# A graph network kernel on one core: a new SBUF layout for the second network's first loads, and an earlier place for a rarely taken branch

## The chip, the cores and the metric

The kernel runs on 1 core of one Trainium2 chip. The metric is the device time of one execution in microseconds. Before the change the median of 3 runs is 2925.94 us (2923.68 to 2931.75). The profile was taken on another execution, which took 2932.24 us; its span, from the first to the last recorded instruction, is 2930.4 us.

## What is computed

The reference runs two networks on 16 graphs (batches b) of 1024 nodes with 128 features. The first network weighs each graph's adjacency by the cosine of the node features; the second thins the adjacency once ("dilation") and runs three layers of a neighbour mean on it, with a normalization over all batches after each layer. Between the two stands a residual and a layer normalization, `h0`.

```python
# first network, three layers
h = h @ W + b
nh = h / max(norm(h), EPS)
h = (edge_weight * (nh @ nh.T)) @ h          # relu but for the last layer
# dilation: row by row over the adjacency, earlier rows' removals count for later rows
row = carry[n]; num = sum(row); rank = cumsum(row)
rm = row & (rank % sf == 0)                  # sf from num
carry[n] = row & ~rm; carry[:, n] &= ~rm
# second network, three layers, adj_d = adj * keep
deg = clip(sum(adj_d, -1), 1)
out = (adj_d @ x / deg) @ Wr + x @ Wx + b
h_l = batchnorm(relu(out / norm(out)))
y = concat(h1, h2, h3) @ Wl + bl             # plus the residual
```

## The kernel before

All batches are held as 8 chunks of 128 nodes (`NCH = 8`), so an adjacency is an 8 by 8 field of 128x128 blocks. The instructions of each engine are put in an order by a scheduler from the program text and its priorities; each engine then works through its own queue in order. SP issues the loads, POOL issues most of the stores.

Stage A, from the start to about 1730 us, is one `ExitStack` (`actx`) with the pools `pool1` ("a1", single buffers) and `pool2` ("a2", double buffers). Two things are woven together in it. `layer0()` (the kernel's name for the first network) works on two batches at a time through three layers; its steps are `products` (cosines times adjacency, L324 to L336), `turn` (transposes, L353), `sums` and `sums_back` (L364, L378), and at a batch's end `residual` (L392, with the DVE operation at L401 and the store of `x2` at L404) and `next_layer` (layer normalization, the store of `h0` at L410). The adjacency of the two batches in work lies in `adjA` (L217). The generator `dilation()` makes the keep masks row chunk by row chunk in a fast form that guesses a number of rounds, and stores them in HBM as `keep` (L720). It also counts in `astray` whether any guess failed. Its tiles (`patt`, `an`, `kl`, `T`, `Z`, `E`, `rank`, `kp` and small ones) are taken from `pool1` and `pool2`, among those of the first network. The driver at L743 weaves the two until `dilation()` ends, with some 7% of the first network left (`SPREAD`).

Then the count is summed (L749 to L754) and each engine loads it into a register (L755, `values_load`). `while step0(): pass` (L766) issues the rest of the first network. After that `tc.If(n_off > 0)` (L768) holds an exact dilation, 16 long loops which run only where a guess failed; with these inputs it isn't taken, so every engine jumps over it. Last come the residual and `h0` of batch 15 (L771, L772).

Stage B, from there on, opens its own pools: "res" (`hR`, the layer's result for all batches), "b2", "br" (the adjacency blocks `aT0` to `aT7`), for its first layer also "bk" (`kb`, the keep mask of a batch, 8 loads of 256 KB into one tile of two buffers; and `both`). A pool of stage B is laid where pools of stage A were, and its first tile waits for what was there.

The first layer of stage B (L908 to L997; called the second layer in the change's name) does for each batch: `fetch` (L913) loads `kb` and `hN` (the batch's `h0`); `weighted` (L791) multiplies it by the weights (`pt_h`, `pw` L803); for each of 8 chunks `masked` (L921) loads the adjacency and its transpose into `aT` (L924, L928), makes the symmetric mask `both` (L933, L935) and applies it (L941, L945), `turn` (L950) transposes the upper blocks and stores `aT` to HBM as `adT` (L960), `Sums.add` (L827) accumulates `agg` (L831). The two other layers (L1040 on) read `adT` back (L1047). The projections of all layers gather in `acc` (L1002), a pool opened after the first layer.

Of the kernel before, what the change touches and what calls it, by code (L numbers as in the profile page):

```python
# [16 lines left out]
P = 128  # L17
# [29 lines left out]
def tile_adj_preln_d2(  # L47
# [47 lines left out]
    GT = 4  # L95
# [73 lines left out]
    with ExitStack() as actx:  # L169
        pool1 = actx.enter_context(tc.tile_pool(name="a1", bufs=1))  # L170
# [5 lines left out]

        w0 = pool1.tile([P, 3, P], F32, name="w0")
# [37 lines left out]


        adjA = pool1.tile([P, 2, base(NCH), P], F32, name="adjA")  # L217
        Nat = {}

        def adj_place(b, q):  # L220
            return adjA[:, b % 2, base(q) : base(q + 1), :]

        def adj_piece(b, q):
            Nat[b, q] = nat = pool2.tile([P, NCH, P], F32, tag="nat", name=f"nat_{b}_{q}")
            nc.sync.dma_start(
                nat[:, : NCH - q, :], adj[b][q * P :, q * P : (q + 1) * P].rearrange("(c p) q -> p c q", p=P)
            )
# [280 lines left out]
        patt = pool1.tile([P, SLOTS, N + 2], F16, name="patt")  # L508
        nc.gpsimd.memset(patt[:, :, 0:2], 0.0)

        astray = pool1.tile([P, BH], F32, name="astray")
        nc.vector.memset(astray, 0.0)

        def thresholds(x, nm):


            th = pool2.tile([P, 2, BH], F32, tag="th", name=f"th_{nm}")
            nc.vector.tensor_scalar(th[:, 0, :], x, EVENS, None, ALU.add)
            nc.vector.tensor_scalar(th[:, 1, :], x, float(T_DIL), LOW, ALU.is_le, ALU.mult)
            return th[:, 0, :], th[:, 1, :]  # L520
# [6 lines left out]
        def dilate(k, half, exact):  # L527
# [8 lines left out]
            left = pool2.tile([P, BH], F32, tag="left", name=f"left{nk}")  # L536
            rest = pool2.tile([P, BH], F32, tag="rest", name=f"rest{nk}")
            if k == 0:
                nc.vector.memset(left, 0.0)
            rbias = pool2.tile([P, BH], F32, tag="rbias", name=f"rbias{nk}")  # L540
            T = pool2.tile([P, BH, P], F16, tag="T", name=f"T{nk}")
            for i in range(BH):
                b = half * BH + i
                an = pool2.tile([P, N], F32, tag="an", name=f"an{nk}_{i}")
                nc.sync.dma_start(an, adj[b, cols, :])
                on = pattern(i)[:, 2 + k * P :]
                nc.scalar.activation(on, an[:, k * P :], AF.Sign)
                nc.scalar.activation(on, on, AF.Relu, accum_out=rest[:, i : i + 1])
                if k:
                    pk = pool2.tile([P, NCH - 1, P], F16, tag="kl", name=f"kl{nk}_{i}")  # L550
                    nc.sync.dma_start(
                        pk[:, :k, :].rearrange("p j q -> p (j q)"), keep_d[b][: k * P, cols], transpose=True
                    )
                    nc.vector.scalar_tensor_tensor(
                        pattern(i)[:, 2 : 2 + k * P],
                        an[:, : k * P],
                        0.0,
                        pk[:, :k, :].rearrange("p j q -> p (j q)"),
                        ALU.is_gt,
                        ALU.mult,  # L560
                        accum_out=left[:, i : i + 1],
                    )
                yield 0.75
                if i % GT == GT - 1:
                    four = range(i - GT + 1, i + 1)
                    bs_ = slice(i - GT + 1, i + 1)
                    pdt = ps_sm.tile([P, GT, P], F16, tag="sm", name=f"pdt{nk}_{i}")
                    for n, ii in enumerate(four):
                        nc.tensor.transpose(pdt[:, n, :], pattern(ii)[:, diag], ident16)
                    dT = pool2.tile([P, GT, P], F16, tag="dT", bufs=1, name=f"dT{nk}_{i}")  # L570
                    nc.scalar.activation(dT, pdt, AF.Copy)
                    nc.vector.tensor_scalar(rbias[:, bs_], rest[:, bs_], 2.0, -2.0, ALU.mult, ALU.add)
                    yield 0.1
                    pT = ps_sm.tile([P, GT, P], F32, tag="sm", name=f"pT{nk}_{i}")
                    for n, ii in enumerate(four):
                        nc.tensor.matmul(pT[:, n, :], lhsT=dT[:, n, :], rhs=upto, start=True, stop=False)
                        nc.tensor.matmul(pT[:, n, :], lhsT=pattern(ii)[:, diag], rhs=off, start=False, stop=False)
                        nc.tensor.matmul(pT[:, n, :], lhsT=ident16, rhs=after, start=False, stop=True)
                    for n, ii in enumerate(four):
                        nc.scalar.activation(T[:, ii, :], pT[:, n, :], AF.Identity, bias=rbias[:, ii : ii + 1])  # L580
                    yield 0.1


            x0 = pool2.tile([P, BH], F32, tag="x0", name=f"x0{nk}")
# [5 lines left out]
            Z = pool2.tile([P, BH, P], F16, tag="Z", name=f"Z{nk}")  # L590
            if ends:
                nc.vector.tensor_scalar(Z, T, 0.0, None, ALU.is_equal)
            else:
                found = pool2.tile([P, 1], F32, tag="found", name=f"found{nk}")
                nc.vector.tensor_scalar(Z, T, 0.0, 0.0, ALU.is_equal, ALU.add, accum_out=found)
                nc.vector.tensor_tensor(astray[:, 0:1], astray[:, 0:1], found, ALU.add)
            E = pool2.tile([P, BH, P], F16, tag="E", name=f"E{nk}")
            par = pool2.tile([P, BH], F16, tag="par", name=f"par{nk}")

            def even(x, nm):  # L600

                ev = pool2.tile([P, BH], F32, tag="ev", name=f"ev_{nm}")
                nc.vector.tensor_scalar(ev, x, EVENS, EVENS, ALU.add, ALU.subtract)
                return ev

            def removals(x, nm):


                if exact:
                    f, low = thresholds(x, nm)  # L610
                    at = pool2.tile([P, 2, BH], F32, tag="at", name=f"at_{nm}")
# [8 lines left out]
                else:  # L620
                    ev = even(x, nm)
                    mid = pool2.tile([P, BH], F16, tag="mid", name=f"mid_{nm}")
# [13 lines left out]
            if exact:  # L636
                x = pool1.tile([P, BH], F32, tag="xe", name=f"xe_{nk}")
# [4 lines left out]
            else:  # L642
                x = x0
                for r in range(ROUNDS[k]):
                    was = x
                    pc = removals(x, f"{nk}_{r}")
                    yield 1.0
                    x = pool2.tile([P, BH], F32, tag="x", name=f"x_{nk}_{r}")
                    nc.vector.tensor_tensor(x, x0, pc, ALU.subtract)
                moved = pool2.tile([P, BH], F32, tag="moved", name=f"moved_{nk}")  # L650
                nc.vector.tensor_tensor(moved, was, x, ALU.not_equal)
                nc.vector.tensor_tensor(astray, astray, moved, ALU.add)
            fin = pool2.tile([P, 3, BH], F32, tag="fin", name=f"fin{nk}")
# [9 lines left out]
            else:  # L663
# [9 lines left out]
                small = pool2.tile([P, BH], F32, tag="small", name=f"small{nk}")  # L673
# [20 lines left out]
            for i in range(BH + 1):  # L694
                if i < BH:

                    pt = pattern(i)
                    ranks[i] = rank = pool2.tile([P, N], F16, tag="rank", bufs=3, name=f"rank{nk}_{i}")
                    nc.vector.tensor_tensor_scan(rank, pt[:, 1 : N + 1], pt[:, 2:], 0.0, ALU.add, ALU.add)  # L699
                    yield 2.5  # L700
# [11 lines left out]
                kp = pool2.tile([P, N], F16, tag="kp", name=f"kp{nk}_{i}")  # L712
# [53 lines left out]
        while step0():  # L766
            pass
        with tc.If(n_off > 0):  # L768
            for _ in dilation(exact=True):
                pass  # L770
        batches[-1].residual()  # L771
# [3 lines left out]
    with ExitStack() as bctx:  # L775
        res = bctx.enter_context(tc.tile_pool(name="res", bufs=1))
        pool2 = bctx.enter_context(tc.tile_pool(name="b2", bufs=2))
        poolr = bctx.enter_context(tc.tile_pool(name="br", bufs=1))
# [129 lines left out]
        with ExitStack() as c1:  # L908
            poolk = c1.enter_context(tc.tile_pool(name="bk", bufs=2))
# [3 lines left out]
            def fetch(b):  # L913
                kb = poolk.tile([P, NCH, N], F16, tag="kb", name=f"kb_{b}")
                for c in range(NCH):
                    nc.sync.dma_start(kb[:, c, :], keep_d[b][c * P : (c + 1) * P, :])
                hN = pool2.tile([P, NCH, D], F32, tag="hN2", bufs=1, name=f"hN1_{b}")
# [3 lines left out]
            def masked(b, q, kb):  # L921
# [10 lines left out]
                for c in range(row):  # L932
                    nc.tensor.transpose(pk[:, c, :], kb[:, q + c, q * P : (q + 1) * P], ident16)  # L933
                both = poolk.tile([P, NCH, P], F16, tag="both", name=f"both_{b}_{q}")
# [3 lines left out]
                    kb[:, q, q * P :].rearrange("p (c q) -> p c q", q=P),  # L938
# [61 lines left out]
        poolc = bctx.enter_context(tc.tile_pool(name="bc", bufs=1))  # L1000
        ps_a = bctx.enter_context(tc.tile_pool(name="b_a2", bufs=2, space=PSUM))
        acc = poolc.tile([P, B, NCH, D], F32, name="acc")  # L1002
# [8 lines left out]
        def project(l, b, hT):  # L1011

            for h in range(NHALF):
# [3 lines left out]
                yield h, pp, acc[:, b, h * CPH : (h + 1) * CPH, :]  # L1017
# [11 lines left out]
        def residual(b):  # L1029
# [3 lines left out]
            for c in range(NCH):  # L1033
# [3 lines left out]
                a = acc[:, b, c, :]  # L1037
# [88 lines left out]
```

## Time and profile before

| what | value |
|---|---|
| median of the runs | 2925.94 us |
| profiled execution: time, span | 2932.24 us, 2930.4 us |
| PE busy | 2673.3 us, 91% of the span |
| DVE busy | 1955.9 us, 67% |
| ACT busy | 1420.2 us, 48% |
| POOL busy | 452.9 us, 15% |
| moved by DMA | 585.21 MB, mean 200 GB/s |
| shares of the chain that ended last | PE 56%, DVE 18%, DMA 13%, issue 6% |

The chain that ended last is followed back from the last instruction, at each step to what released it. PE leads it, but the share is a mean over stages with different limits: each stage has to be read from its own windows. "Idle before" in a row of the timeline is the time that the engine stood before this instruction, with the instruction that ended it; a name with q (SPq, PEq, DVEq) is an engine's sequencer. The granted clock (PEclk) is a share of TensorE's full clock.

### The profile page before, as it was taken

To read this page: it belongs to the slowest core of one execution; us is meant where nothing else is said; L and a number is where in the kernel's file an instruction comes from. 1 tells how busy PE (TensorE), PEld (TensorE's weight loads), DVE (VectorE), ACT (ScalarE), POOL (GpSimd) and SP (SyncE) were. 2 spreads that over 40 slices of the span, in tenths; PEclk is the share of its full clock that TensorE was granted. 3 is DMA by queue.
4 is the path that set the end of the run, shared out by engine and by line. 5 is a ranking of instruction groups with operands and counts; after the bars stand their busy time and mean duration, and the time that the engine had idled before them with its cause. 6 is when DMAs were issued, how large, how long until landed. Compare 5 with 4: busy or idle time off the path is not lost.

```text
span 2930.4 us, 51972 instructions
## 1 busy us (share of the span) xinstructions
PE 2673.3 (91%) x18803; PEld 2205.6 (75%) x18803; DVE 1955.9 (67%) x4945; ACT 1420.2 (48%) x4069; POOL 452.9 (15%) x604
## 2 busy tenths in 40 slices
PE   5898998998989989998998979999989999899996
PEld 3666666666666666766666758989979999899996
DVE  2777778877977878788778446777772233455555
ACT  5766667557546546455455323333333333333333
POOL 2111112012011112121112002222220010010010
PEclk9999999999999999999999989999999999999998
DMA  8437258247347456386162039999995666576763
GB/s 268 145 115 219 89 168 247 77 139 229 92 130 219 105 169 188 95 248 176 39 206 105 1 114 403 405 406 404 405 372 173 208 210 202 177 243 222 240 217 115
DMA packets 383017, 585.21 MB, mean 200 GB/s; under 512 B 85201, under 2 KB 267345, under 8 KB 382753
## 3 DMA queue, kind: packets, MB, share of 16 engines
q1 hardware_dynamic: 343280, 425.28, 45.9%
q0 software_dynamic: 38464, 156.07, 14.4%
q8 instruction: 151, 2.47, 0.3%
q14 instruction: 114, 0.93, 0.1%
q10 hardware_dynamic: 1008, 0.46, 0.1%
HBM read 403.44 MB, written 163.58 MB: 193 GB/s over the span
## 4 chain that ended last, share of the span: by engine, by line
PE 56%; DVE 18%; DMA 13%; issue 6%; ACT 4%; POOL 1%; SPq 1%; POOLq 0%; DVEq 0%; another core or an unknown queue 0%; ACTq 0%
PE agg L831 20%; PE po L364 7%; PE pg L324 6%; DVE rank L699 5%; PE pw L803 5%; PE po L378 5%; DVE ew L336 4%; DMA aT<-in_adj_dram 3%; PE gt L353 3%; PE pp L1016 2%; DMA kl<-keep 2%; PE pw L273 2%; DMA an<-in_adj_dram 2%; DMA aT<-adjT 1%; DMA kb<-keep 1%
## 5 line engine op out<-in xcount | busy, mean ns | idle before, releaser
L831 PE MATMUL agg<-hw,aT 128*128 128x128 f32 (+1 forms) x6144 | 742.9, 277 | 8.8 <-DVE aT L941 7.5
L831 PEld LDWEIGHTS agg<-hw,aT 128*128 128x128 f32 x6144 | 712.1, 192 | 14.7 <-DVE aT L941 10.1
L324 PE MATMUL pg<-nhT 128*128 128x512 f32 (+3 forms) x1152 | 457.4, 500 | 71.9 <-DVE ew L336 63.0
L364 PE MATMUL po<-ew,hS 128*128 128x512 f32 (+3 forms) x1152 | 455.3, 499 | 13.8 <-ACT hTo L387 9.9
L336 DVE TENSOR_TENSOR ew<-pg,adjA 128x768 f32<-128x768 f32 (+3 forms) x528 | 425.1, 827 | 4.6 <-DVEq L768 2.7
L378 PE MATMUL po<-ew,hS 128*128 128x128 f32 x2688 | 366.9, 277 | 0.0
L378 PEld LDWEIGHTS po<-ew,hS 128*128 128x128 f32 x2688 | 339.3, 193 | 36.6 <-issue 36.3
L354 ACT ACTIVATE ew<-gt 128x512 f32<-128x512 f32 (+1 forms) x480 | 208.9, 465 | 243.2 <-PE gt L353 240.2
L324 PEld LDWEIGHTS pg<-nhT 128*128 128x128 f32 x1152 | 188.7, 193 | 171.6 <-issue 120.9
L699 DVE TENSOR_TENSOR_SCAN rank<-patt 128x1024 f16<-128x1024 f16 x128 | 294.0, 2307 | 0.9
L364 PEld LDWEIGHTS po<-ew,hS 128*128 128x128 f32 x1152 | 195.8, 194 | 105.6 <-issue 72.9
L353 PEld LDWEIGHTS gt<-ident,ew 128*128 128x128 f32 x1344 | 167.8, 143 | 97.3 <-issue 68.5
L333 DVE TENSOR_TENSOR ew<-pg,adjA 128x128 f32<-128x128 f32 x384 | 108.1, 282 | 196.3 <-PE pg L324 150.9
L353 PE MATMUL gt<-ident,ew 128*128 128x128 f32 x1344 | 212.1, 277 | 4.1 <-ACT ew L354 2.7
L881 POOL TENSOR_TENSOR o<-o,rn 128x512 f32<-128x512 f32 x96 | 107.6, 1121 | 650.4 <-DVE rn L880 646.0
L803 PE MATMUL pw<-wrx,hT 128*128 128x256 f32 x768 | 181.1, 391 | 10.2 <-ACT hT L1006 9.7
L805 DVE TENSOR_TENSOR own<-pw,bs 128x256 f32<-128x256 f32 x192 | 81.4, 424 | 148.0 <-ACT hw L804 148.0
L803 PEld LDWEIGHTS pw<-wrx,hT 128*128 128x128 f32 x768 | 146.3, 196 | 32.7 <-ACT hT L1006 10.5
L959 ACT ACTIVATE aT<-pta 128x512 f32<-128x512 f32 (+3 forms) x160 | 71.2, 466 | 205.0 <-PE pta L958 178.0
L860 DVE SCALAR_TENSOR_TENSOR o<-agg,invdeg,own 128x128 f32<-128x128 f32 x384 | 109.7, 344 | 87.0 <-PE agg L831 78.3
L876 ACT ACTIVATE own<-o 128x128 f32<-128x128 f32 x384 | 114.6, 301 | 103.3 <-DVE o L860 103.2
L301 POOL TENSOR_TENSOR hS<-hN,rn 128x1024 f32<-128x1024 f32 x48 | 94.6, 1970 | 409.2 <-DVE rn L157 300.4
(161 smaller groups left out, 3962.2 us busy)
## 6 DMA issues: line engine op xcount, KB each, us to landing
an<-in_adj_dram SPq DMA_DIRECT2D x128, 512.0 KB, 4.6
keep<-kp POOLq DMA_DIRECT2D x128, 256.0 KB, 3.6
kb<-keep SPq DMA_DIRECT2D x128, 256.0 KB, 5.4
aT<-adT SPq DMA_DIRECT2D x32, 960.0 KB, 5.4
aT<-adT SPq DMA_DIRECT2D x32, 832.0 KB, 5.5
aT<-adT SPq DMA_DIRECT2D x32, 704.0 KB, 4.6
aT<-adT SPq DMA_DIRECT2D x32, 576.0 KB, 3.4
xb<-in_x_dram SPq DMA_DIRECT2D x31, 512.0 KB, 5.1
```

The costliest lines, as they stand in the source:

```text
L324: nc.tensor.matmul(pg[:, :n, :].rearrange("p c q -> p (c q)"), lhsT=self.nhT[:, q * P : (q + 1) * P], rhs=self.nhT[:, (q + c) * P : (q + c ...
L333: nc.vector.tensor_tensor(ew[:, 0, :], pg[:, 0, :], place[:, 0, :], ALU.mult)
L336: nc.vector.tensor_tensor(both[0][:, :, off, :], pg[:, own:n, :].unsqueeze(1).to_broadcast([P, 2, n - own, P]), both[1][:, :, off, :], ALU ...
L353: nc.tensor.transpose(pt[:, i, :], ew[:, at + i, :], ident)
L354: nc.scalar.activation(ew[:, at : at + n, :], pt[:, :n, :], AF.Copy)
L364: nc.tensor.matmul(self.po[:, c * P : (c + n) * P], lhsT=self.hS[:, q, :], rhs=ew[:, c - q : c - q + n, :].rearrange("p c q -> p (c q)"), ...
L378: nc.tensor.matmul(self.po[:, q * P : (q + 1) * P], lhsT=self.hS[:, q + n, :], rhs=ew[:, NCH - 1 - q + n, :], start=False, stop=closes and ...
L699: nc.vector.tensor_tensor_scan(rank, pt[:, 1 : N + 1], pt[:, 2:], 0.0, ALU.add, ALU.add)
L803: nc.tensor.matmul(pw[:, i, :], lhsT=hT[:, 2 * h + i, :], rhs=wrx[:, l, :], start=True, stop=True)
L831: nc.tensor.matmul(self.place(c), lhsT=aT[:, blk, :], rhs=self.hw[:, source, :], start=source == 0 and c % self.ga == 0, stop=ends(c, source),
L860: nc.vector.scalar_tensor_tensor(self.o[:, c, :], self.place(c)[:, :P], invdeg[:, b, c : c + 1], self.own[:, c, :], ALU.mult, ALU.add,)
L876: nc.scalar.activation(self.own[:, n, :], self.o[:, n, :], AF.Square, accum_out=ss[:, c : c + 1])
```

## The change

Five edits:

- A pool `poold` ("ad") is opened ahead of `pool1`, and all tiles of the dilation, and `nat` (the adjacency pieces before they are transposed), move to it.
- `adjA` becomes two tiles, one for even and one for odd batches, and stands first in `pool1`.
- In stage B the order of the pools is turned: "bc" first, then "br", "b2" and "res". `acc` becomes 16 tiles `acc0` to `acc15` of "bc", and the first layer's `kb` (now four tiles of two chunks for each batch), `hN` and `both` take turns with them under the same tags. The pool "bk" is gone.
- The loop that issues the rest of the first network is cut in two: 12 steps, then the branch to the exact dilation, then the remaining steps.
- The final residual's tile `x2f` no longer shares its buffer with `hN`.

```diff
     with ExitStack() as actx:
+        poold = actx.enter_context(tc.tile_pool(name="ad", bufs=2))
         pool1 = actx.enter_context(tc.tile_pool(name="a1", bufs=1))
...
+        adjA = [pool1.tile([P, base(NCH), P], F32, name=f"adjA{i}") for i in range(2)]
...
-        adjA = pool1.tile([P, 2, base(NCH), P], F32, name="adjA")
...
-            Nat[b, q] = nat = pool2.tile([P, NCH, P], F32, tag="nat", name=f"nat_{b}_{q}")
+            Nat[b, q] = nat = poold.tile([P, NCH, P], F32, tag="nat", name=f"nat_{b}_{q}")
...
-        patt = pool1.tile([P, SLOTS, N + 2], F16, name="patt")
+        patt = poold.tile([P, SLOTS, N + 2], F16, bufs=1, name="patt")
...
-        while step0():
-            pass
+        for _ in range(12):
+            step0()
         with tc.If(n_off > 0):
             for _ in dilation(exact=True):
                 pass
+        while step0():
+            pass
         batches[-1].residual()
         batches[-1].next_layer()
...
+        poolc = bctx.enter_context(tc.tile_pool(name="bc", bufs=1))
+        poolr = bctx.enter_context(tc.tile_pool(name="br", bufs=1))
+        pool2 = bctx.enter_context(tc.tile_pool(name="b2", bufs=2))
         res = bctx.enter_context(tc.tile_pool(name="res", bufs=1))
-        pool2 = bctx.enter_context(tc.tile_pool(name="b2", bufs=2))
-        poolr = bctx.enter_context(tc.tile_pool(name="br", bufs=1))
...
             def fetch(b):
-                kb = poolk.tile([P, NCH, N], F16, tag="kb", name=f"kb_{b}")
+                two = [
+                    poolc.tile([P, 2, N], F16, tag=f"acc{b % 2 * (NCH // 2) + i}", name=f"kb{i}_{b}")
+                    for i in range(NCH // 2)
+                ]
+                kb = [two[c // 2][:, c % 2, :] for c in range(NCH)]
                 for c in range(NCH):
-                    nc.sync.dma_start(kb[:, c, :], keep_d[b][c * P : (c + 1) * P, :])
-                hN = pool2.tile([P, NCH, D], F32, tag="hN2", bufs=1, name=f"hN1_{b}")
+                    nc.sync.dma_start(kb[c], keep_d[b][c * P : (c + 1) * P, :])
+                hN = poolc.tile([P, NCH, D], F32, tag=f"acc{NCH}", name=f"hN1_{b}")
...
-                both = poolk.tile([P, NCH, P], F16, tag="both", name=f"both_{b}_{q}")
+                both = poolc.tile([P, NCH, P], F16, tag=f"acc{NCH + 1 + q % 2}", name=f"both_{b}_{q}")
...
-        poolc = bctx.enter_context(tc.tile_pool(name="bc", bufs=1))
...
-        acc = poolc.tile([P, B, NCH, D], F32, name="acc")
+        acc = [poolc.tile([P, NCH, D], F32, tag=f"acc{b}", name=f"acc{b}") for b in range(B)]
```

The other tiles of the dilation move from `pool2` to `poold` line by line in the same way.

## The prediction

> **What bounds the kernel now.** I read the page's slices first, then windows at the seam between the two networks, then what SP waited for there, then the branch's own rows.
>
> Part 2 of the page, 73.3 us to a slice:
>
> ```profile
> PE   5898998998989989998998979999989999899996
> DMA  8437258247347456386162039999995666576763
> GB/s 268 145 115 219 89 168 247 77 139 229 92 130 219 105 169 188 95 248 176 39 206 105 1 114 403 405 406 404 405 372 173 208 210 202 177 243 222 240 217 115
> ```
>
> From the 25th slice on the rate stands at 403 to 406 GB/s for five slices: the first layer of the second network is bound by transfers. Just before it the rate falls to 1 GB/s while PE is at 9: the first network's end is bound by PE and leaves the DMA engines empty. Windows (busy us of PE, PEld, DVE, ACT, POOL, then granted clock, DMA share, GB/s):
>
> ```profile
> 1650.00:1700.00 50.00, 49.88 (x289) 36.90 (x288) 22.65 (x53) 16.26 (x57) 3.79 (x2) 1.00 0.00 1
> 1730.00:1742.00 12.00, 6.73 (x24) 5.43 (x24) 4.11 (x23) 5.69 (x14) 1.93 (x4) 0.60 0.52 173
> 1800.00:2160.00 360.00, 344.05 (x2967) 324.79 (x2966) 273.61 (x650) 139.62 (x479) 94.01 (x147) 1.00 1.04 406
> ```
>
> So loads started earlier shorten the transfer-bound stage only by DMA time now empty, and PE time lost before the seam delays everything. What holds the loads, by SP's waits in 1690 to 1800 and SP's timeline:
>
> ```profile
> SPq L918 <- DVE x L401: 20.4, 1, 20.4
> SPq L916 <- DMA h<-h: 4.8, 1, 4.8
> ...
> 1565.74 0.37 SPq L253 DMA_DIRECT2D xb<-in_x_dram  x1
> 1730.67 6.82 SPq L918 DMA_DIRECT2D hN<-h  x2
> 1742.78 3.67 SPq L916 DMA_DIRECT2D kb<-keep  x8
> ```
>
> SP issues nothing for 165 us. `hN` then goes when batch 15's last residual (L401) is done, `kb` 12.11 us later, when batch 15's `h0` has been stored.
>
> **The layout.** It is meant to let `kb` go as soon as the branch is passed, since `kb` lies over `patt`. In the built program it doesn't: the first `kb` load waits for the last L401 of batch 15, the last `sums_back` matmul and the last ew copy, exactly the set for which `hN` waits now. Waits between pools are taken for whole pools, it seems: "bc" occupies bytes 25088 to 90624, "ad" ends at 90368 and "a1" begins there, so "bc" overlaps "a1" by 256 bytes and inherits the wait for all of it. So the loads start at the old `hN` place, 1730.67 plus what the branch moves. It is a gain all the same, because the wait for the stored `h0` is gone: 12.11 us earlier. In these 12 us the DMA engines moved 173 of a possible 406 GB/s, two `hN` loads and two stores of 0.52 MB each, which in the new order must share the transfer-bound time. Gain (406 - 173) / 406 x 12.11 = **6.9 us**. Ends: 12.1 if latency and not bytes paces the stage; about 4 if the new order (`hN` behind eight `kb` loads, so `pw` and `agg` of batch 0 come later) leaves a hole of 3 us. I expect none: the loads that need no free buffer come to 9.2 MB, 23 us at 406 GB/s, and batch 0's first block should be stored by then.
>
> **The rest of the layer.** `kb` in four tiles comes free piece by piece, and SP's queue has `kb` spread among the `aT` loads. At 406 GB/s and a share of 1.04 this buys nothing: 0, hidden by the transfers themselves. Splitting `adjA` and moving the dilation's tiles: up to the branch the built program has the same instructions in the same order with the same waits on every engine; 0. `x2f` alone in its buffer: one load that was in this layer already; 0.
>
> **The branch at its old place.** Its rows, and PE's beside it:
>
> ```profile
> L768 PEldq COMPARE_BRANCH  x1: 3419/3419/3419, 1707.3 to 1707.3; - x1
> L768 DVEq COMPARE_BRANCH  x1: 76/76/76, 1709.4 to 1709.4; - x1
> L768 DVEq EVENT_SEMAPHORE  x1: 21/21/21, 1712.3 to 1712.3; - x1
> ...
> 1710.87 1.10 PE L364 MATMUL po<-ew,hS 128*128 128x512 f32 x2 [0.78 <-PEq L768]
> 1713.55 0.89 PE L324 MATMUL pg<-nhT 128*128 128x384 f32 x2 [1.14 <-DVE ew L336]
> ```
>
> The jump costs each engine about 3 us to its next instruction (DVE 1709.4 to 1712.3, PE 3.42). PE felt little, since its queue held 3 us of matmuls: 0.78 us by itself and 1.14 through DVE. Taking it away saves **1.9 us** (0 if the tail's own chain takes it up, 2.7 if all of DVE's idle time there goes).
>
> **The branch at its new place.** Each engine's register load (L755) now stands right before it. PE's was at 1706.7, long after the value was ready; now it waits for the cast at L754, which ends at 1608.02. In the built program only one instruction (two records, 0.26 us) of this row stands between:
>
> ```profile
> 1608.30 1.28 PE L378 MATMUL po<-ew,hS 128*128 128x128 f32 x10
> ```
>
> PE is done with its queue at 1608.56; load 0.48 and jump 3.42 end at 1612.0. PE stands for **3.4 us** in a stretch with no slack. Queued behind are the rest of L378, L324 and all that DVE and ACT make of them; DVE's and ACT's own jumps end within the same time. POOL takes about 4.5 us over load, jump and semaphores (1690.6 to 1695.1 now) and must await the last `keep` store, issued 1605.97; its next work, the multiplication at 1634.90, covers that. SP has nothing to issue and covers its own. Here a rule speaks against the row. The Trainium skill, "Advanced Engine Details and Errata", Control Flow Timing, prices a compare-and-branch at about 108 ns; by that PE would stand for only 0.2 us and the whole sum would be 5.4 us better. The rows show 3 us on five engines, so I take the row. Ends: 0.2 and 5, as now all five jump at once.
>
> Then the clock. After an idle time like that PE ran at half clock earlier in this trace, a 3.63 us gap before 702.89:
>
> ```profile
> 702.00:704.00 2.00, 1.11 (x5) 1.11 (x6) 0.00 (x0) 2.00 (x6) 0.00 (x0) 0.52 1.11 356
> 704.00:706.00 2.00, 2.00 (x7) 1.43 (x7) 0.93 (x2) 0.73 (x2) 0.00 (x0) 0.50 0.09 29
> 706.00:708.00 2.00, 2.00 (x5) 0.82 (x4) 1.88 (x11) 1.07 (x8) 0.55 (x1) 0.50 0.22 86
> 708.00:710.00 2.00, 2.00 (x16) 2.00 (x15) 2.00 (x14) 0.77 (x2) 0.00 (x0) 0.78 0.12 45
> ```
>
> Half for some 6 us is 3 us lost; the gaps before 879.55 and 1377.45 (3.73 and 3.52 us) cost 1.7 and 1.9, counted alike. Gaps of 2.2 to 2.4 us before 232.69 and 979.99 cost nothing. The Trainium skill, "TensorE: Matmul & The Clock Gate", What's actually happening, halves the clock after an idle window of about 3.4 us and restores it after a busy one as long, which would be 1.7 us or, at a gap of just 3.4, perhaps nothing. I take the mean of the three rows, **2.2 us**; ends 0 and 3.
>
> **The sum.** -6.9 - 1.9 + 3.4 + 2.2 = -3.2 us. Layers two and three and the end come later by nothing and sooner by that. Against the profiled 2932.24 us (span 2930.4 and 1.84 around it) that is 2929.0; the median of the runs is 6.3 lower, so 2925.94 - 3.2 = **2922.7 us**.
>
> **Rivals.**
> 1. The branch costs little, or the stage takes the whole 12.1 us. With gains 12.1 and 1.9 and costs of at most 2, -12 us: 2914. For it: PE's queue hid most of the jump before, and the first batch has latency chains. Against: flat 406 GB/s, and the queue is empty at the new place.
> 2. The loads really start behind the branch near 1612. Then `kb` and `hN` of batch 0 and `kb` of batch 1, 4.7 MB or 11.6 us, leave the stage as well, perhaps some `aT`: -15 to -26, about 2905. For it: the intention and 100 us of empty DMA. Against: the waits in the program.
> 3. Slower: the jump at 1608 to 1612 is the one place. If five jumps at once make it 6 us, PE also loses 3 at half clock, 9 together, and it decides once it exceeds the 8.8 us that the seam and the old place give back. With the hole of 3 us in the first batch it is 9 - 5.9 = +3, 2929; to be slower by more than 9 us the jump would have to take about 12. For it: nothing hides this stop. Against: SP, alone in 1608, took as long as the three that jumped together in 1707 to 1712.
>
> **How the numbers follow.** Forecast 0.57, with its own range 2918 to 2927 (-8 to +1); rival 1 0.23; rival 2 0.09; rival 3 0.11. A change under 0.3%, 8.8 us, can't be told from none. Rivals 1 and 2 lie beyond it, less a little of rival 1, plus a little of the forecast: faster 0.33. Slower by 0.3% is the far half of rival 3: 0.05. The rest, 0.62, is no change. Leaving 0.09 below (rival 2) and 0.07 above or so, the range is 2910 to 2931.
>
> **What would show it.** In the profile after: the first `kb` load on SP right after the last L401 of batch 15 and not before 1725 us; a gap of 3 to 4 us on PE near 1609 with a clock near 0.5 behind it; none of PEq at 1710; 173 GB/s at the seam gone; still 406 after it; the same pace of some 27 us a batch. Wrong would be: `kb` loads at 1615, PE running through 1610, or a rate that leaves 406.

## The result and the profile after

Over 20 runs the changed kernel takes 2931.55 us (median; 2922.5 to 2942.37), the kernel before 2929.55 us (2919.28 to 2935.49): a ratio of 1.0014, with a 95% interval of 1.0004 to 1.0025. That is 4.1 us slower, and clear of zero, where 3.2 us faster had been forecast. (The ratio isn't the quotient of the medians, which are 2.0 us apart; the means are 4.0 us apart.)

The profiled execution took 2939.14 us with a span of 2937.4 us, well above its own median, so its surplus of 7.0 us over the span before is partly scatter. I cut both traces at events that both have: the matmul that sums the count (at 1606 us), the start of the last DVE operation in batch 15's residual, the issue of the last `adT` store of the second network's first layer, and the end.

| stretch (us) | before | after |
|---|---|---|
| start to the count | 1606.3 | 1606.0 |
| count to the last residual of batch 15 (the tail) | 123.8 | 127.2 |
| from there to the last `adT` store (the first layer) | 456.8 | 458.5 |
| from there to the end | 743.5 | 745.7 |

The tail lost 3.4 us, as the branch's cost led one to expect. But the first layer, which was to give 6.9 us back, became longer instead. (The last stretch, 2.2 us longer, lies at the edge of the scatter: 742.8 to 745.7 us in all eleven profiles.) First what went as forecast. SP's timeline of the changed kernel (start, us, engine, line, operation, count):

```profile
1565.39 0.37 SPq L255 DMA_DIRECT2D xb<-in_x_dram  x1
1733.71 5.01 SPq L925 DMA_DIRECT2D kb<-keep  x8
1738.77 0.43 SPq L927 DMA_DIRECT2D hN<-h  x1
```

The loads still wait for the end of the first network: the last DVE operation of batch 15's residual starts at 1733.2 and the first `kb` load goes half a microsecond later. It is 9.1 us earlier than before and no longer waits for the stored `h0`. PE's timeline at the branch's new place:

```profile
1612.31 2.05 PE L380 MATMUL po<-ew,hS 128*128 128x128 f32 x8 [3.97 <-PEq L770]
```

The 3.97 us are the stop that was forecast as 3.4. Now windows of the changed kernel (busy us of PE, PEld, DVE, ACT, POOL; granted clock, DMA share, GB/s):

```profile
1606.00:1636.00 30.00, 25.91 (x138) 18.87 (x138) 10.39 (x24) 6.19 (x18) 2.06 (x2) 0.94 0.04 13
1650.00:1700.00 50.00, 49.77 (x280) 36.27 (x279) 23.18 (x56) 16.60 (x57) 3.79 (x2) 1.00 0.01 1
1730.00:1742.00 12.00, 3.11 (x19) 1.62 (x19) 4.69 (x26) 4.03 (x10) 1.93 (x4) 0.71 0.61 202
1800.00:2160.00 360.00, 337.40 (x2902) 319.39 (x2901) 267.48 (x643) 135.58 (x463) 92.28 (x143) 0.99 1.04 399
1820.00:1880.00 60.00, 49.85 (x414) 46.96 (x413) 39.71 (x100) 18.85 (x64) 12.36 (x21) 0.91 1.00 363
```

The last two rows hold the surprise. The layer's rate has fallen from 406 to 399 GB/s, and the loss sits in one place, 1820 to 1880 us, where the rate is 363 and PE is busy for 49.85 of 60 us with its clock at 0.91. The kernel before in the same window:

```profile
1820.00:1880.00 60.00, 57.38 (x498) 54.19 (x497) 45.44 (x105) 22.41 (x75) 16.88 (x25) 1.00 1.04 406
```

(406 - 363) / 406 x 60 = 6.4 us of transfers are missing. A fallen rate alone would not name the cause: in a later run, the kernel before with only the branch moved, the rate was 377 GB/s in 1800 to 1860 while PE was busy for 58.40 of the 60 us. Here PE stands. The timeline of all engines:

```profile
1819.32 1.53 DVE L954 SCALAR_TENSOR_TENSOR aT<-aT,both 128x512 f32<-128x512 f32 x1
...
1821.74 0.38 SPq L1040 DMA_DIRECT2D x2f<-x  x1
...
1831.25 0.61 DVE L1042 SCALAR_TENSOR_TENSOR x2f<-blb,mf,x2f 128x128 f32<-128x128 f32 x2 [10.41 <-DMA x2f<-x]
1831.78 0.42 DVE L944 TENSOR_TENSOR both<-pkb,kb 128x512 f16<-128x512 f16 x1
...
1833.63 0.87 PE L967 MATMUL pta<-ident,aT 128*128 128x128 f32 x3 [8.56 <-issue]
...
1837.57 0.83 SPq L925 DMA_DIRECT2D kb<-keep  x2
```

Read it from the third row on. DVE stands for 10.41 us in front of L1042, the first operation of the final residual (its load is L1040), which belongs to the third layer, hundreds of microseconds later. It waits for a load that SP issued only after DVE had come to a stop, and that took 9.5 us to land among the layer's other transfers. Behind L1042 in DVE's queue stands the mask product L944 of the layer itself. Without it PE has no masked blocks to turn (8.56 us of idle time) and no `adT` store is issued between 1822.51 and 1836.68. SP goes on with loads until 1829.81; then it issues none until a `kb` tile has come free, at 1837.57. The same tile's rows in the kernel before (duration ns min/median/max, first and last start; then who it waited for, us and times):

```profile
L1032 SPq DMA_DIRECT2D x2f<-x x16: 370/384/1222, 2166.1 to 2831.2; - x16
  DMA x2f<-x: 52.3, 15
```

and in the changed one:

```profile
L1040 SPq DMA_DIRECT2D x2f<-x x16: 370/384/1026, 1821.7 to 2836.8; - x16
  DMA x2f<-x: 60.8, 16
```

Before, the first `x2f` load went at 2166 us, at the layer's end: its buffer was `hN`'s, and batch 15's `hN` had to be read first. In the changed kernel `hN` has moved to "bc", nothing holds `x2f` back, and the scheduler has put both the load and the DVE operations into batch 2's time, 88 us after the first `kb` load. There is one wait more (16 for 15) and 8.5 us more of them.

### The profile page after: what moved, and what is told of

It reads as the page before. It is cut to its first block, busy times and chain, and to the rows that moved or that the text cites. A ratio compares the mean times of both kernels' runs of the same rounds, so it can differ in the third digit from the quotient of the medians.

```text
span 2937.4 us, 51964 instructions
## 1 busy us (share of the span) xinstructions
PE 2675.7 (91%) x18803; PEld 2207.9 (75%) x18803; DVE 1950.6 (66%) x4945; ACT 1420.2 (48%) x4069; POOL 453.1 (15%) x604
```

## The experiments

The theory (A): the layout alone gains about what was forecast, the branch costs a few microseconds, and the freed `x2f` puts a wait of 10 us into DVE's queue that costs the layer 6 to 8 us. The main rival (B): the stop is covered by transfers that are due anyway, and the new order or the four pieces of `kb` cost the time. Ratios are to the kernel before; 0.001 is 2.9 us. Quotients of the pooled means differ from them by up to 0.0009. The tail and the first layer are those of the table above, each from one profile.

| kernel | ratio (95% interval) | tail | first layer |
|---|---|---|---|
| the changed kernel | 1.0014 (1.0004 to 1.0025) | 127.2 | 458.5 |
| `x2f` held back | 0.9990 (0.9974 to 1.0005) | 127.9 | 450.3 |
| branch at its old place | 1.0007 (0.9994 to 1.0019) | 124.4 | 457.1 |
| both of these | 0.9983 (0.9973 to 0.9993) | 126.0 | 453.5 |
| the kernel before, branch moved | 1.0005 (0.9987 to 1.0023) | 125.3 | 461.8 |
| early `x2f` load, late DVE operations | 0.9992 (0.9976 to 1.0008) | 127.9 | 451.4 |
| dilation's pool longer | 0.9963 (0.9948 to 0.9977) | 126.8 | 439.9 |
| the same, `x2f` held back | 0.9942 (0.9921 to 0.9963) | 126.9 | 437.4 |
| the same, branch later | 0.9942 (0.9923 to 0.9960) | 128.3 | 436.9 |
| the same, `adjA0` in its own pool | 0.9931 (0.9911 to 0.9950) | 128.5 | 435.2 |

**`x2f` held back.** One line of the changed kernel is undone:

```diff
-                hN = poolc.tile([P, NCH, D], F32, tag=f"acc{NCH}", name=f"hN1_{b}")
+                hN = pool2.tile([P, NCH, D], F32, tag="hN2", bufs=1, name=f"hN1_{b}")
```

> The kernel after, with one line undone: hN of the second network's first layer shares its buffer with x2f again, so that the first x2f load can't be issued before the last batch's hN has been read. Theory A (the early x2f load stops VectorE for 10.4 us, TensorE for 8.6 us and lets the transfer rate fall below 406 GB/s for some 60 us, worth 6.4 us of transfers): the x2f load goes back to about 2165 us, the rate is 403 to 412 GB/s in every 20 us between 1800 and 2140, and the time is 6 us below the changed kernel's, 2 us below the kernel before (ratio about 0.9992). Rival B (the stop is covered by the transfers that are due anyway, and the loss comes from the new order of the loads, or from kb in four pieces): the time stays at 1.0014 and the rate is again below 406 in some stretch.

The load goes back to 2160.7 us, and the window of the gap is whole again:

```profile
1820.00:1880.00 60.00, 57.65 (x502) 54.70 (x502) 45.89 (x111) 23.89 (x82) 14.74 (x23) 1.00 1.04 407
```

The ratio falls to 0.9990, by 7.0 us, and the layer to 450.3 us. A is borne out, B is not; with the two intervals taken as independent the 7.0 us are uncertain by 5.4. One expectation missed a little: the rate in each 20 us between 1800 and 2140 was 400 to 413, where 403 to 412 were named.

**The branch at its old place,** the rest as changed:

```diff
-        for _ in range(12):
-            step0()
+        while step0():
+            pass
         with tc.If(n_off > 0):
             for _ in dilation(exact=True):
                 pass
-        while step0():
-            pass
```

> The kernel after, with the branch put back behind the last step of the first network; the new layout and the free x2f stay. If the branch's new place costs what the two profiles show at the seam (the first load 3.0 us later than where hN went before), the time is 3 us below the changed kernel's: ratio about 1.0004. If the place of the branch costs nothing in sum (the new stop and the old one cancel), it stays at 1.0014. If the early place is what releases the loads, it is slower than the changed kernel.

1.0007: 2.1 us below the changed kernel, by an interval that would also allow nothing. The tail is short again (124.4 us) and the first `kb` load keeps its place behind the last residual. So the early place, by itself, released no load. The `x2f` stop is there in this kernel too, though shorter: the load goes at 1809.5, DVE stands for 6.78 us in front of the first `x2f` operation and PE for 4.93.

**Both undone together,** so that only the layout stays:

> The kernel after with both undone: x2f held back by hN's buffer and the branch behind the first network's last step. Only the new layout stays. Theory A: from the count's matmul to the first network's end as in the kernel before (124 us); from there to the last adT store 450 us as in the run with x2f held (457 in the kernel before); so 6.5 to 7 us below the kernel before, ratio 0.9977. Rival (early x2f and late branch are of one cause, or the layout alone brings nothing): 1.0000 or above.

0.9983: the layout alone is 5.0 us faster (2.1 to 7.9), somewhat less than the 6.5 to 7 expected; in its profile the tail took 126.0 us and the layer 453.5, where 124 and 450 had been named. With the other two it makes a square: holding `x2f` is worth 7.0 us with the branch early (1.0014 to 0.9990) and 7.0 us with it late (1.0007 to 0.9983; uncertain by 4.7).

**The kernel before, with only the branch moved,** by the same edit as the change's:

> The kernel before, with only the branch moved behind 12 steps of the first network's rest. Theory A: TensorE stands for 4.0 us near 1608 with half the clock for some us behind it, the two small stops at 1707 go; the first hN load is 3 us later than in the kernel before, and so is the end: ratio 1.0010. Rival: the tail takes the stop up, ratio 1.0000; or the stop grows as five engines jump at once, 6 us or more, ratio 1.002.

1.0005, 1.5 us, between the two expectations and told apart from neither by its interval. PE's gap is 3.62 us. Its first layer, 461.8 us, is 5 us longer than before's without any part of the change being in it: the layer's first batches scatter by that much from one execution to another, which is why I trust the ratios more than single profiles.

**The early load with late DVE operations.** In the changed kernel the mask column that L1042 reads for batch 0 is passed through a tile that depends on the first layer's normalization (`ab1`); its values stay the same:

```diff
+            m = mf[:, b, :]
+            if b == 0:
+                z = pool2.tile([P, 1], F32, bufs=1, name="z0")
+                nc.vector.tensor_scalar(z, ab1[:, 0:1], 0.0, None, ALU.mult)
+                m = pool2.tile([P, NCH], F32, bufs=1, name="mf0")
+                nc.vector.tensor_scalar(m, mf[:, 0, :], z, None, ALU.add)
...
-                    x2[:, c, :], blb[:, 0, :], mf[:, b, c : c + 1], x2[:, c, :], ALU.mult, ALU.add
+                    x2[:, c, :], blb[:, 0, :], m[:, c : c + 1], x2[:, c, :], ALU.mult, ALU.add
```

> The kernel after with one thing changed: VectorE's first x2f operations take their mask column through a tile that depends on the first layer's normalization, so that they stand at that layer's end in VectorE's queue. The early x2f load stays where the changed kernel has it on SP, among the kb loads of batch 4. Theory A (the cost is VectorE standing at the head of its own queue for a load that was issued 0.9 us after it got there): no idle time of 10 us on VectorE and TensorE near 1831, 403 to 412 GB/s between 1800 and 2140, time as with x2f held, ratio about 0.999. Rival (the extra load in SP's queue, or the kb loads held up behind it, cost the time): 1.0014 as the changed kernel, with the rate below 400 near 1840.

The rows of `x2f` in this kernel, and its window:

```profile
L1049 DVE SCALAR_TENSOR_TENSOR x2f<-blb,mf,x2f x128: 342/346/353, 2190.6 to 2832.4; 128x128 f32<-128x128 f32 x128
...
L1047 SPq DMA_DIRECT2D x2f<-x x16: 370/384/1202, 1819.4 to 2825.5; - x16
```
```profile
1820.00:1880.00 60.00, 56.96 (x499) 54.28 (x499) 45.01 (x111) 23.77 (x82) 14.82 (x24) 1.00 1.05 404
```

The load is as early as in the changed kernel (1819.4), the operations are late (2190.6), and the loss is gone: 0.9992, and 451.4 us for the layer. The rate in each 20 us was 395 to 412 GB/s, a little below the 403 named in four of them, with 400 at 1820, where the changed kernel had 369, and 408 at 1840, where it had 339. So it is not the extra load, nor its place among the `kb` loads, but the waiting operation at the head of DVE's queue. The gain over the changed kernel, 6.4 us, is uncertain by 5.6.

**The dilation's pool longer,** so that "bc" ends below "a1"; nothing else:

```diff
-        astray = poold.tile([P, BH], F32, bufs=1, name="astray")
+        astray = poold.tile([P, BH + 72], F32, bufs=1, name="astray")[:, :BH]
```

> The kernel after, with the dilation's pool made 288 bytes longer for each partition, so that the pool bc of the second network ends below the first network's tiles. If those 256 bytes of overlap are what holds the first loads, kb and hN of batch 0 and kb of batch 1 are issued at about 1612 us instead of 1734; 4.7 MB, 11.6 us at 406 GB/s, leave the transfer-bound layer, and with the x2f stop still there the time is 11.6 us below the changed kernel's: ratio about 0.9974. Rival: the loads start early, but the first aT and hT, which still wait for the first network's end, set the pace, so that only some 5 us come out: 0.9996. If the overlap is not what holds them, 1.0014.

SP's timeline, and the longest of its waits between 1600 and 1745 us (us in total, times, longest):

```profile
1606.60 3.67 SPq L925 DMA_DIRECT2D kb<-keep  x8
1610.32 0.47 SPq L927 DMA_DIRECT2D hN<-h  x1
1610.83 113.68 SPq L925 DMA_DIRECT2D kb<-keep  x10
```
```profile
SPq L925 <- DVE both L944: 105.9, 1, 105.9
```

The 256 bytes were what held the loads. `kb` and `hN` of batch 0 and `kb` of batch 1 now go right behind the branch; then SP waits 105.9 us for the first buffer that the layer itself must free. The ratio is 0.9963, 15 us below the changed kernel (10 to 20), where 11.6 us of bytes were expected. And the `x2f` stop has all but gone without being touched: the load goes at 1770.5, in DVE's queue the first `x2f` operation stands three masking operations later within its batch than in the changed kernel, DVE waits for 1.25 us, and PE for no more than 0.74.

**The same with `x2f` held back** (256 bytes now, and only the last batch's `hN` in `x2f`'s buffer):

```diff
+                if b < B - 1:
+                    hN = poolc.tile([P, NCH, D], F32, tag=f"acc{NCH}", name=f"hN1_{b}")
+                else:
+                    hN = pool2.tile([P, NCH, D], F32, tag="hN2", bufs=1, name=f"hN1_{b}")
```

> The kernel after with the dilation's pool 256 bytes longer, and x2f held back until the last batch's hN has been read (that hN alone lies in x2f's buffer). Against the longer pool alone (0.9963; x2f stop at 1770 us, transfer rate 354 GB/s over 20 us there) it should gain what that stop cost: at least the 2.6 us of transfers missing in those 20 us, at most the 8 us that it was worth in the changed kernel: ratio 0.9935 to 0.9955. If the stop is free when the loads are early, 0.9963.

0.9942, 6 us below, inside the expected range, but the interval (7.5 us to either side) allows nothing too. The expectation took it that the longer pool's kernel still had the stop; with 1.25 us of it left there, these 6 us are not shown to be the stop's cost. This kernel is 17 us faster than the kernel before (11 to 23).

**The branch later, behind 28 steps instead of 12:**

```diff
-        for _ in range(12):
+        for _ in range(28):
```

> As the run with the longer pool and x2f held, but with the branch behind 28 steps instead of 12: 65 matmuls more of TensorE's row stand between the count's cast and its register load, some 14 us, so that TensorE no longer waits for the value and comes to the jump with a filled queue. Theory A (it was the wait for the value that emptied the queue): TensorE's gap at the branch falls from 3.6 to 4.0 us to between 0.8 and 2.5, as at the old place, the clock stays, and the stretch from the count to the first network's end falls from 127 to 124 us; 2 to 3 us below that run. Rival (the jump costs TensorE its 3.5 us wherever it stands early): no change.

The gap at the branch fell to the expected size, and the time did not. PE's timeline:

```profile
1625.32 1.67 PE L366 MATMUL po<-ew,hS 128*128 128x384 f32 x4
1629.03 0.63 PE L355 MATMUL gt<-ident,ew 128*128 128x128 f32 x4 [2.04 <-PEq L770]
1631.98 0.47 PE L355 MATMUL gt<-ident,ew 128*128 128x128 f32 x1 [2.32 <-issue]
```

After its own 2.04 us PE turns four blocks and stands again for 2.32 us. What held it then is not shown: the profile names no releaser ("issue"). DVE and ACT came out of their own jumps at 1629.17 and 1629.35, but DVE's product was over at 1629.86 and ACT's copy at 1630.35, 1.6 us before PE went on, so their lateness can't fill the whole gap. The next kernel below has the same pair, 2.32 and 2.29 us. The filled queue hid a part of PE's jump and a second stop took it back. The tail was 128.3 us, no shorter than the 126.9 without the later place: the rival's number came, though its reason (one stop of 3.5 us) did not.

**`adjA` of the even batches in its own pool,** below the `aT` tiles:

```diff
+        poolj = actx.enter_context(tc.tile_pool(name="aj", bufs=1))
         pool1 = actx.enter_context(tc.tile_pool(name="a1", bufs=1))
...
-        adjA = [pool1.tile([P, base(NCH), P], F32, name=f"adjA{i}") for i in range(2)]
+        adjA = [(poolj, pool1)[i].tile([P, base(NCH), P], F32, name=f"adjA{i}") for i in range(2)]
```

> As the run with the later branch, but with adjA of the even batches in a pool of its own, exactly below the aT tiles of the second network. The aT loads of batch 0 then wait for batch 14's last products alone, some 15 us ahead of the first network's end, not for all of its tiles: 4.19 MB, 10.3 us at 406 GB/s, move into the empty stretch. If the layer is still bound by transfers: 8 to 10 us below the run with the later branch, ratio 0.990 or somewhat lower. Rival (with kb already there TensorE, 95% busy in the layer, takes over as the bound): less than 4 us.

A miss: the `aT` loads of batch 0 do go early, at 1693 to 1704 us, but the gain is 3 us (0.9931 against 0.9942, within the intervals) and 1.7 in the layer's length. SP's waits between 1700 and 1745 us, and the windows of this kernel at the end of the first network:

```profile
SPq L926 <- DVE both L948: 30.3, 2, 23.0
```
```profile
1700.00:1720.00 20.00, 19.88 (x109) 14.18 (x108) 11.52 (x41) 6.31 (x16) 0.95 (x1) 1.00 0.42 146
1720.00:1740.00 20.00, 18.10 (x140) 15.72 (x139) 13.75 (x41) 10.51 (x26) 3.01 (x6) 1.00 0.38 107
```

With all buffers of the first batches full, SP waits 23 us for DVE to use up a `kb` tile of batch 0, which needs the first network's engines to be free. The bytes moved earlier, and a new hole opened behind them (107 GB/s, where the kernel with the branch later has 128 without the earlier bytes); from 1740 to 1780 the rate is 382 to 383 GB/s, where that kernel has 404 to 406. The wait is for a free buffer; whether more buffers would bring the 10 us was not tried.

## Why the prediction was wrong

- **What bounds the kernel, and what holds the loads:** right. The tail is bound by PE, the layer by transfers. The built program's wait, and the 256 bytes behind it, were confirmed by the longer pool: 1606.60 us instead of 1733.71.
- **The layout, -6.9 us:** right in kind, and near in size. Alone it measured -5.0 (-7.9 to -2.1). The rate in 1730 to 1742 rose to 202 GB/s, no more, as the first load goes out only at 1733.71; behind that stand 392 GB/s in 1740 to 1760 (329 before) and, the other way, 357 in 1760 to 1780 (403 before). From 1730 to 1800 it is 354 for 340: 1.0 MB more, worth 2.4 us at 406 GB/s, though the first network ended 3.1 us later. By this estimate the seam gave 5.5 us. No run parts the seam from the layout's other pieces.
- **"`x2f` alone in its buffer: one load that was in this layer already; 0."** This is the step that failed. Two comparisons with `x2f` held back (0.0024 each) and the one with late DVE operations (0.0022) put it at 6 to 7 us. Each is uncertain by some 5 us, and each is clear of zero; two of them share the changed kernel. (By pooled means they would be 7.9, 4.7 and 6.4 us.) I counted the load and its bytes. I did not ask what `hN`'s buffer had been holding back, nor where the operations that consume the load stand in DVE's queue. What the runs show in its place is a wait of 10.41 us on DVE and 8.56 on PE in the middle of the layer. The order of DVE's queue can be read in the built program, where I had read only the waits of the first loads.
- **The rest of the layer, `kb` in four pieces, 0:** nothing speaks against it; with `x2f` held back the layer runs at 406 GB/s between 1800 and 2140.
- **The branch away from its old place, -1.9:** the two kernels that keep it there in the new layout show PE gaps of 2.52 and 2.66 us (PE's record of the jump there is 4.99 and 5.13 us, not 3.42), so it was sized a little low.
- **The branch at its new place, +3.4, and the clock, +2.2:** the gap was 3.97 us here and 3.61 to 3.67 in the five other runs with this place. The price of about 108 ns in the Trainium skill, "Advanced Engine Details and Errata", Control Flow Timing, would have missed it: PE's record of the jump is 3.84 us at the new place. The clock's term is looked at below. In sum the move was taken as +3.7 and measured smaller: 2.1, 2.1 and 1.5 us in three comparisons, none clear of zero alone, and by the tails of nine profiles 127.0 (six with 12 steps) against 124.7 (three at the old place), 2.3 us.
- **The rivals:** the slower case was given for a jump of 6 us; slower came, but by another mechanism, in a place that no rival named. Of the prediction's own signs of being wrong it was the last, a rate that leaves 406, that came.

The measured terms, layout -5.0, `x2f` +7.0 and branch +2.1, make the measured +4.1 us by construction, as they are the steps from one kernel to the next. What the runs add is that the `x2f` step is the same in both orders, and that the branch moved alone gives 1.5. With 7.0 in place of the 0, the prediction's own terms would have given -3.2 + 7.0 = +3.8. That this comes so near is partly luck: it had the layout's gain 1.9 us too large and the branch's cost 1.6 too large, and the two cancel. The named 2922.7 us also started from a median of three runs, 3.6 us below the 20-run median of the same kernel.

Two things stay open. The longer pool brought 15 us where 4.7 MB account for 11.6. The interval (10 to 20) covers 11.6, and the stop that shrank from 10.41 to 1.25 us could account for the rest; no run parts the two. And what the shared buffer is worth where the stop is nearly gone (6 us, give or take 7.5) isn't known.

## What to carry to other kernels

A shared buffer is also an order. Before you free a tile, ask which load its buffer was holding back, where a scheduler will put that load and its consumers once nothing holds them, and what stands behind the first waiting consumer in its engine's queue: 10 us at the head of DVE's queue cost a transfer-bound layer some 7, though the load itself was nearly free, and in the kernel with the longer pool the same wait was 1.25 us. And when pools are laid over each other, compare their ends byte by byte: 256 bytes of overlap made the first loads wait for the whole next pool, and taking them away was worth more than the rest of the change.

## What the runs showed of the hardware that was not expected

The clock behind a stop of the same length differs from run to run. Windows of 30 us from the count on, of the kernel before with the branch moved (gap 3.62 us):

```profile
1603.60:1633.60 30.00, 26.27 (x148) 19.02 (x148) 11.95 (x30) 7.36 (x27) 2.08 (x2) 1.00 0.04 13
```

and of the kernel with early load and late DVE operations (the same branch place, PE busy for the same 26.2 us):

```profile
1601.00:1631.00 30.00, 26.24 (x132) 18.48 (x132) 10.49 (x24) 6.19 (x19) 2.07 (x2) 0.89 0.04 13
```

The first kept its full clock, the second lost 0.11 x 30 = 3.3 us of it, and the changed kernel, with a gap of 3.97 us, lost 1.8. So in these runs the term lies anywhere between 0 and 3.3 us for a stop near 3.6 us, and a mean of earlier rows is the best that can be said. Shorter stops differ too: at the branch's old place one of 2.52 us left a clock of 1.00 over the tail's last 25 us, and one of 2.66 us left 0.93. Two stops of 2.04 and 2.32 us close behind one another, in the kernel with the later branch, left a clock of 0.91 over their 30 us.

The tails follow the clock. Of the six with 12 steps, the one that kept 1.00 took 125.3 us, the three at 0.94 took 126.8 to 127.2, and the two at 0.89 took 127.9. With the lost clock taken off (the six lose 2.0 us in the mean, the three at the old place 0.7), the means are about 125 and 124 us. By this estimate, from nine profiles, about 1 us of the branch's 2.3 is its place and the rest is the clock that the stop happened to cost.
